# Spreading the queries by products, and drawing the scores by halves of the keys, in a fused convolution and attention kernel

## The chip, the cores and the metric

The kernel runs on one core of a Trainium2 chip. The metric is device time in microseconds (us), the median of three runs. A profile of one further execution shows every instruction, and its time stands beside its span below. The engines are TensorE (PE, matmuls; its weight loads are shown as PEld), VectorE (DVE), ScalarE (ACT), GpSimd (POOL) and SyncE (SP, which here only issues transfers). PSUM is the memory that PE writes, SBUF the working memory of the other engines, DRAM the large one outside.

## What is computed

Eight images of 32 x 32 places with 256 channels pass through two layers. Layer 0, cut to what matters here:

```python
conv_out = conv3x3(gn(x)) + conv_b                       # 192 of 256 channels
kqv = gn(x) @ qkv_w + qkv_b                              # k, q, v of 64 channels each, 8 heads of 8
logits = q @ k.T + rel_w(q, key_rel_w) + rel_h(q, key_rel_h)
weights = softmax(logits)                                # 1024 x 1024 per head
attn = (weights @ v) @ attn_w + attn_b                   # the other 64 channels
x = x + concatenate([conv_out, attn])
```

`rel_w` and `rel_h` add to each logit a number that depends on the query and on the distance of the key's column, or row, from the query's. Layer 1 is an attention over 1024 tokens (U = 128) with layer norm, and then a pair of experts for each image (a routed feed-forward network with gelu and a second norm).

## The kernel before

**Units.** Layer 0's attention of an image is worked in four units. A unit is one group of four heads (`g`) with one half of the 512 queries (`half`). For each unit the kernel builds a tile `F` in SBUF of 128 rows by 2 x 4 x 512 elements: for each half `a` of the keys, each head and each query, the features whose product with the key rows `KM` gives the whole logit, relative terms included. Rows 0 to 95 of `F` come from the DRAM scratch `fd` (the same for both `a`), 32 rows from the scratch `fy` (different for each `a`). Two further rows, `R_M` and `R_M + 32`, take the negated maxima in two parts, so that the logit less its maximum leaves PE ready for Exp.

A unit goes through `score` (32 products `lg` of 128 queries with 512 keys, each followed by a DVE maximum into `mx`), `fold`, `fold_in` and `fold_out` (the two halves' maxima become one, are transposed as `pmx`, and four ACT transfers `F<-mb` put them into F), `weigh` (32 products `st`, each followed by an Exp on ACT into `PT`) and `gather` (products `po` with the values). One `weigh` is a *place*; an image has 128 places, four units of 32. While unit n is weighed, the next unit is scored, paced by `starts`: for units 0 to 2 place p asks for p*4/3 + 1 scores, for unit 3, which scores the first unit of the next image, for (p - 5)*8/5 + 1. Place 25 folds, place 28 sends the maxima.

**Order around it.** The order on each engine is the order in which the program is written (`manual_schedule`); each engine works in that order. Other work is threaded in by `Fill`: `chains` are generators that move one step (to their next `yield None`) at each place, and `dense` holds the convolution's products `pc`, sent at the rate that `pace` gives: work still owed over the places left until place 88 of the image whose convolution runs (`LAST`). `second_layer(b - 1)` stands between units 0 and 1 of image b, `project(b - 1)` as a chain in unit 0.

**The path to a next image's first F.** `normalise(b)` makes `kq`, and from it `kqh`: a rounded high part and the low rest. When `may_query` allows (unit 2's first place) it stores the keys' rows (`kd`), and `queries(b)` fills `qs`: for each group, rows of the high part twice and of the low part twice, by eight transfers from `kqh` on SP; four more store query rows into `fd`; POOL copies `qs` into `qx` with rows and columns of the image exchanged. `keys` loads the key rows into `KM`. Then the products for the values (`pvv`), five empty places, and `features`: four `column` and four `row` products (`prel`, eight matmuls each) with a high and a low part each, stored into `fd` (`store_columns`) and `fy`. `Unit(b, 0)` then asks SP for F: both `fd` loads first, then four `fy` loads. `qs`, `qx` and the rows' buffers lie in `scr`, which has the same slot as that unit's F. The next `Unit(b, 1)` is asked for at unit 3's first place. For image 0 the same path runs at the start with nothing beside it, `taps` (the convolution's weights) and the 32 scores of unit 0 behind it.

Lines that the steps touch: L561 (the eight transfers), L568 (query rows into `fd`), L573 (`qx`), L581 (`keys`), L484 to L500 (`pvv` and empty places), L612 and L634 (`prel` parts), L620 and L641 (stores), L712 to L719 (F), L725 (`score`), L765 (`F<-mb`), L845 (`aT`) and L865 (`ns`), L927 (`pace`), L941 (`starts`). Products through the counting helper all carry L133.

Of the kernel before, what the change touches and what calls it, by code (L numbers as in the profile page):

```python
# [38 lines left out]
def kernel(  # L39
# [72 lines left out]
    with ExitStack() as ph:  # L112
# [59 lines left out]
        brow = work.tile([1, 2 * CO], FP, tag="n", name="brow", bufs=2)[:, 0 : 4 * DK].rearrange("p (a o) -> p a o", a=2)  # L172
        nc.scalar.dma_start(out=brow[:, 0], in_=qkv_b[0 : 2 * DK].rearrange("(o p) -> o p", o=1))
        M = 2 * HH - 1
        rawt = {}
        for n, table in (("h", key_rel_h), ("w", key_rel_w)):
            rawt[n] = wp.tile([M, DH], FP, tag=f"raw{n}", name=f"raw{n}")
            nc.scalar.dma_start(out=rawt[n], in_=table)
# [4 lines left out]
        nc.scalar.dma_start(out=l0b[:, 0, CO:C], in_=attn_b.partition_broadcast(P))  # L183
        rawc = f_tile("rawc", 2, FP).rearrange("p a h s -> p (a h s)")[:, 0 : 9 * KC * CO]
        nc.sync.dma_start(
# [7 lines left out]
        bo = wp.tile([P, 1, C], FP, tag="bo", name="bo")  # L193

        kqs = wp.tile([P, 1], FP, tag="kqs", name="kqs")
        nc.gpsimd.memset(kqs[0:DK, :], 1.0)
        nc.gpsimd.memset(kqs[DK : 2 * DK, :], DH**-0.5)
        gsel = wp.tile([P, P // GSIZE], FP, tag="gsel", name="gsel")
        nc.vector.tensor_reduce(gsel, ident.rearrange("p (g d) -> p g d", d=GSIZE), AX.X, ALU.add)
# [4 lines left out]
        gavg = gavg.rearrange("p g d -> p (g d)")  # L204
        hsel = wp.tile([P, HG], FP, tag="hsel", name="hsel")
        nc.vector.tensor_reduce(hsel, ident.rearrange("p (c h) -> p h c", h=HG), AX.X, ALU.add)
# [196 lines left out]
        def normalise(b):  # L403
# [70 lines left out]
            nc.sync.dma_start(out=kds[b % 2].rearrange("l p s -> p l s"), in_=kqb_[0:DK])  # L474
            qs, qx, scr = queries(b)
            if b == 0:
                for g in range(NG):
                    keys(b, g, nc.scalar)
            else:
                keys(b, 0)  # L480
            for g in range(2):
                nc.gpsimd.tensor_tensor(T[b][g], T[b][g], l0b.to_broadcast([P, 4, C]), ALU.add)
            v0[b] = work.tile([P, NT, DK], FP, tag="v0", name="v0")
            for g in range(2):  # L484
# [13 lines left out]
                yield None  # L498
            for _ in range(5):
                yield None  # L500
            yield from features(b, qs, qx, scr)
            units[b, 0] = Unit(b, 0)
            while b > 0 and (done[b - 1] < NT or not may_combine.get(b)):
                yield None
            yield from combine(b, base)

        may_query, may_combine, units = {}, {}, {}
        v0 = {}

# [43 lines left out]

        def queries(b):
            kqb_ = ready.pop(b)
            scr = f_tile("scr", b % 2).rearrange("p w h s -> p (w h s)")
            qs = scr[:, 0 : 2 * S].rearrange("p (g s) -> p g s", g=NG)
            qx = scr[:, 2 * S : 4 * S].rearrange("p (g s) -> p g s", g=NG)
            for i in range(4):
                for g in range(NG):  # L560
                    nc.sync.dma_start(  # L561
                        out=qs.bitcast(FP)[32 * i : 32 * i + 32, g],
                        in_=kqb_[DK + 32 * g : DK + 32 * g + 32, i // 2, :],
                    )
            fd = fds[b % 2]
            for g in range(NG):
                for c in range(2):
                    nc.sync.dma_start(  # L568
                        out=fd[g].rearrange("(l c p) s -> c p l s", c=2, p=32)[c, :, 0:2],
                        in_=kqb_[DK + 32 * g : DK + 32 * g + 32],  # L570
                    )
            for g in range(NG):
                nc.gpsimd.tensor_copy(  # L573
                    qx[:, g].rearrange("p (x y) -> p y x", y=HH), qs[:, g].rearrange("p (y x) -> p y x", x=WW)
                )
            return qs, qx, scr

# [8 lines left out]
        def features(b, qs, qx, scr):  # L586
# [49 lines left out]

            def store_columns():
                for g in range(NG):
                    dst = fds[b % 2][g][R_M * HG : (R_M + 64) * HG].rearrange("(l p) s -> p l s", p=P)
                    for p in (slice(HG, 64), slice(64, P)):  # L640
                        nc.sync.dma_start(out=dst[p], in_=whole[g].bitcast(FP)[p])  # L641

# [3 lines left out]
            for q in range(3):  # L646
                row(q)
                yield None
            yield None
            store_columns()  # L650
            yield None
# [50 lines left out]
        class Unit:  # L702


            def __init__(self, b, n):
                self.g, self.half = divmod(n, 2)
                g, cols = self.g, slice(self.half * 512, self.half * 512 + 512)
                self.F = f_tile("F", 2 if n == 3 else (b + n) % 2)
                self.Fb = self.F.bitcast(FP)
                fd = fds[b % 2][g].rearrange("(r h) s -> r h s", h=HG)  # L710
                for a in range(2):
                    nc.sync.dma_start(out=self.Fb[0 : R_M + 64, a], in_=fd[:, :, cols])  # L712
                for l in range(2):
                    r = R_Y + 16 * l
                    for a in range(2):
                        nc.sync.dma_start(
                            out=self.Fb[r : r + 16, a],
                            in_=fys[b % 2][g][l, 64 * a : 64 * a + 64, cols].rearrange("(i h) s -> i h s", h=HG),
                        )  # L719
                self.mx = work.tile([P, 2, 4, HG], FP, tag="mx", name="mx", bufs=2)  # L720
                self.scored = self.gathered = 0
                self.pts = {}
                self.po = None

            def score(self):  # L725

                n, a = divmod(self.scored, 2)
                i, hl = divmod(n, HG)
# [107 lines left out]
        def project(b, sec, half, gaps):  # L836
# [6 lines left out]
            for j, t in enumerate(ts):  # L843
                te.transpose(tp[0:DK, j * P : (j + 1) * P], at[:, t, :], ident)
            aT = work.tile([DK, 512], FP, tag="aT", name="aT")  # L845
            nc.scalar.copy(aT, tp[0:DK])
# [15 lines left out]
            for _ in range(gaps[1]):  # L862
                yield None

            ns = pt_tile("n")[:, 0 : 4 * C].rearrange("p (j c) -> p j c", c=C)  # L865

# [56 lines left out]
        def pace(b, place):  # L923

            left = (LAST if done.get(b, NT) < NT else 128 + LAST) - place  # L927
            return fill.owed / max(left, 1)
# [8 lines left out]
        def first_layer(b):  # L937


            more = b + 1 < B  # L940
            starts = [lambda p: p * 4 // 3 + 1] * 3 + [lambda p: (p - 5) * 8 // 5 + 1]  # L941
            for s in range(NU * NT):
# [29 lines left out]
                for p in range(HG):  # L972
                    place = 4 * j + p
                    unit.weigh(j, p)
                    if nxt in units:
                        u = units[nxt]
                        while u.scored < min(32, starts[n](place)):
                            u.score()
# [494 lines left out]
```

## Time and profile before

| | us |
|---|---|
| median of 3 runs (2437.92 to 2442.56) | 2438.52 |
| the profiled execution | 2442.88 |
| its span | 2441.1 |
| PE busy in the span | 2179.2 |
| DVE busy | 1406.7 |
| ACT busy | 1031.7 |
| first score | 94.65 |
| first `weigh` of image 0 | 131.26 |
| first `weigh` of image 7 | 1668.17 |
| first experts' matmul | about 1972 |

How to read it: the span has a start of 131 us, eight images of about 227 us each (some 102 of them in unit 0 with the second layer, and 41 to 44 in each other unit), an end of the second layer for the last image, and from about 1956 us the experts, which the change does not touch. An instruction's line gives its start and length; in square brackets is the engine's idle time before it and what ended it. `SPq` and `ACTq` are the issues of transfers by these engines.

### The profile page before, as it was taken

The numbers are of one execution on the slowest core, as the hardware profiler recorded it, in microseconds if no ns is written. First come the engines' busy times: TensorE is split into PE (matmuls) and PEld (weight loads), VectorE is DVE, ScalarE is ACT, GpSimd is POOL, SyncE is SP. The second block draws the span as 40 slices with busy tenths as digits, with TensorE's granted clock in tenths as the row PEclk, the third lists the DMA queues.
The fourth block names the chain that finished last, engine by engine and source line by source line (L and its number), as shares of the span: only waits on it lengthen the run. The fifth ranks groups of instructions, "written<-read, shape, count | busy, mean of one in ns | idle before, by whom it ended". The sixth has DMA issues, their size and how long they took to land.

```text
span 2441.1 us, 28659 instructions
## 1 busy us (share of the span) xinstructions
PE 2179.2 (89%) x10507; PEld 1402.5 (57%) x10507; DVE 1406.7 (58%) x3141; ACT 1031.7 (42%) x1969; POOL 501.9 (21%) x430
## 2 busy tenths in 40 slices
PE   4579899989999999899899999989997789999998
PEld 3446456645655665566456555655653556666665
DVE  4647657665767577567657675767571533333333
ACT  1135443554455445545543554455364322222332
POOL 2211220212031122302120311032011042222220
PEclk7689999999999999999999999999998989999999
DMA  4624512441371255025512532370120121121210
GB/s 115 148 66 93 129 36 70 121 79 36 78 173 19 44 113 138 11 65 123 116 36 70 141 59 44 75 176 10 44 44 1 51 93 70 69 69 69 79 51 26
DMA packets 92317, 185.97 MB, mean 76 GB/s; under 512 B 9441, under 2 KB 37994, under 8 KB 90642
## 3 DMA queue, kind: packets, MB, share of 16 engines
q1 hardware_dynamic: 90368, 181.55, 30.8%
q10 hardware_dynamic: 1810, 2.59, 0.5%
q8 instruction: 84, 1.38, 0.3%
q14 instruction: 55, 0.45, 0.1%
HBM read 112.15 MB, written 62.52 MB: 72 GB/s over the span
## 4 chain that ended last, share of the span: by engine, by line
PE 68%; DVE 16%; DMA 7%; ACT 5%; issue 2%; SPq 1%; ACTq 1%; POOL 1%; DVEq 0%; POOLq 0%
PE po L133 12%; PE phd L1383 9%; PE py L1400 9%; PE lg L133 9%; PE st L133 8%; DVE mx L738 6%; PE pc L133 5%; DMA F<-fy 3%; PE pq L133 3%; PE prel L133 2%; DMA F<-mb 2%; PE tp L137 2%; ACT PT L782 2%; PE pa L133 1%; PE pv L133 1%
## 5 line engine op out<-in xcount | busy, mean ns | idle before, releaser
L738 DVE TENSOR_REDUCE mx<-lg 128x1 f32<-128x512 f32 x1024 | 657.2, 683 | 282.8 <-PE lg L133 274.9
L782 ACT ACTIVATE PT<-st 128x512 f32<-128x512 f32 x1024 | 596.2, 598 | 474.8 <-PE st L133 426.4
L133 PE MATMUL st<-F,KM 128*128 128x512 f32 x1024 | 518.7, 510 | 46.6 <-ACT PT L782 30.6
L133 PE MATMUL lg<-KM,F 128*128 128x512 f32 x1024 | 384.0, 414 | 59.8 <-DMA F<-fy 49.3
L133 PEld LDWEIGHTS st<-F,KM 128*128 128x128 f32 x1024 | 196.6, 193 | 263.3 <-ACT PT L782 195.4
L133 PE MATMUL po<-PT,vk 128*32 128x512 f32 x2048 | 281.9, 621 | 0.0
L133 PE MATMUL pc<-convw,V 128*128 128x192 f32 x1152 | 264.0, 335 | 6.7 <-ACT mm L681 5.7
L133 PEld LDWEIGHTS lg<-KM,F 128*128 128x128 f32 x1024 | 196.3, 192 | 102.4 <-issue 58.1
L133 PEld LDWEIGHTS pc<-convw,V 128*128 128x128 f32 x1152 | 214.2, 196 | 48.5 <-issue 11.9
L1383 PE MATMUL phd<-n2T,w 128*128 128x512 f32 x512 | 225.4, 596 | 0.0
L1400 PE MATMUL py<-w,hT 128*128 128x256 f32 x1024 | 223.6, 379 | 0.0
L1400 PEld LDWEIGHTS py<-w,hT 128*128 128x128 f32 x1024 | 194.6, 190 | 33.3 <-issue 7.7
L1407 DVE TENSOR_TENSOR r<-py,n 128x256 f32<-128x256 f32 x64 | 27.2, 424 | 259.8 <-PE py L1400 259.8
L1383 PEld LDWEIGHTS phd<-n2T,w 128*128 128x128 f32 x512 | 96.2, 191 | 114.1 <-issue 110.4
L687 POOL TENSOR_TENSOR ms<-mm 128x192 f32<-128x192 f32 x32 | 19.1, 598 | 665.2 <-ACT mm L681 665.2
L1018 DVE TENSOR_REDUCE nm<-lg 128x1 f32<-128x512 f32 x128 | 85.8, 686 | 113.8 <-PE lg L133 113.8
L1022 ACT ACTIVATE pr<-lg,nm 128x512 f32<-128x512 f32 x128 | 86.8, 683 | 128.8 <-DVE nm L1019 128.6
L1390 ACT ACTIVATE hT<-phd,b1c 128x512 f32<-128x512 f32 x128 | 86.3, 686 | 96.6 <-PE phd L1383 96.4
L133 PE MATMUL lg<-nqk 128*128 128x512 f32 x256 | 120.8, 595 | 0.0
L133 PE MATMUL po<-pt,v 128*128 128x256 f32 x512 | 115.8, 379 | 0.0
L133 PEld LDWEIGHTS po<-pt,v 128*128 128x128 f32 x512 | 95.1, 190 | 11.6
L1343 POOL TENSOR_SCALAR w<-w,wbc 128x1024 f32<-128x1024 f32 x16 | 45.9, 2871 | 251.1 <-DMA w<-in_L_ffn_W_dram 249.3
(251 smaller groups left out, 2459.5 us busy)
## 6 DMA issues: line engine op xcount, KB each, us to landing
F<-fd SPq DMA_DIRECT2D x64, 768.0 KB
F<-fy SPq DMA_DIRECT2D x128, 128.0 KB
w<-in_L_ffn_W_dram SPq DMA_DIRECT2D x32, 512.0 KB
fy<-scr SPq DMA_DIRECT2D x48, 256.0 KB
T<-in_x_dram SPq DMA_DIRECT2D x16, 512.0 KB
scr<-kqh SPq DMA_DIRECT2D x64, 128.0 KB
fd<-kqh SPq DMA_DIRECT2D x32, 256.0 KB
fd<-rel SPq DMA_DIRECT2D x16, 512.0 KB
```

The lines of the kernel that those rows point to most:

```text
L133: nc.tensor.matmul(out, **kw)
L137: nc.tensor.transpose(out, in_, ident)
L687: nc.gpsimd.tensor_tensor(ms, mm[:, 0], mm[:, 1], ALU.add)
L738: nc.vector.tensor_reduce(self.mx[:, a, i, hl : hl + 1], lg, AX.X, ALU.max, negate=True)
L782: nc.scalar.activation(self.pts[j][:, hl, :], st, AF.Exp)
L1018: nc.vector.tensor_reduce(nm[:, h : h + 1], lg[h], AX.X, ALU.max, negate=True)
L1022: nc.scalar.activation(pr[:, h * 512 : (h + 1) * 512], lg[h], AF.Exp, bias=nm[:, 2:3], scale=scale, accum_out=rs[:, h, i : i + 1],)
L1343: nc.gpsimd.tensor_scalar(w2t, w2t, wbc[:, n : n + 1], None, ALU.mult)
L1383: nc.tensor.matmul(phd, lhsT=ws[k][0][:, kc, f * P : (f + 1) * P], rhs=n2T[:, kc, q * 512 : (q + 1) * 512], start=kc == 0, stop=kc == KC - 1,)
L1390: nc.scalar.activation(hT[:, k * NF + f, :], phd, AF.Gelu, bias=b1c[:, f, k * B + b : k * B + b + 1])
L1400: nc.tensor.matmul(py, lhsT=hT[:, k * NF + f, j * P : (j + 1) * P], rhs=ws[k][1][:, f, :], start=k + f == 0, stop=k == TOPK - 1 and f == N ...
L1407: nc.vector.tensor_tensor(r[:, j, :], py, n2[:, q * 4 + j, :], ALU.add)
```

## The change

The eight transfers that spread the queries' rows are replaced by PE products. A constant `twice` (128 x 192) holds for each of the two groups' 32 rows two identity blocks in columns 64 to 127 and zero elsewhere; used from column 64 it puts the high part into output rows 0 to 63, used from column 0 it puts the low part into rows 64 to 127, both summed in one PSUM tile `pqs`. ACT copies `pqs` into `qs`. `queries` becomes a generator of two steps, and its stores into `fd` come ahead of the products. `pvv` moves into `values`, which for image 0 runs after its first unit's F is asked for, and for the others after `queries`; the five empty places become one. For image 0 the column stores go to ACT's queue after row 0, and the keys' loads come, also on ACT, after F is asked for.

F is asked for by halves of the keys (`fd` and two `fy` loads for `a = 0`, then the same for `a = 1`), and `score` draws all 16 products of the first half ahead of the second's. Unit 3's scores are paced as those of the other units. For the last image `pace` spreads the convolution until place 120. Four small constants and the tables' raw rows move into free space of `rawc`, and `aT` into the `pt` slot that `ns` takes later, so that slot is taken from the start of `project`.

```diff
+        twice = wp.tile([P, 192], FR, tag="twice", name="twice")
+        for c in (0, 64):
+            nc.vector.tensor_scalar(twice[:, c : c + P], ident, 0.0, None, ALU.mult)
+        for g in range(NG):
+            r = slice(DK + 32 * g, DK + 32 * g + 32)
+            for i in range(2):
+                nc.vector.tensor_copy(twice[r, 64 + 32 * i : 96 + 32 * i], ident[r, r])
...
-            qs, qx, scr = queries(b)
-            if b == 0:
-                for g in range(NG):
-                    keys(b, g, nc.scalar)
-            else:
-                keys(b, 0)
+            yield from queries(b)
+            qs, qx, scr = spread.pop(b)
+            if b > 0:
+                keys(b, 0)
             for g in range(2):
                 nc.gpsimd.tensor_tensor(T[b][g], T[b][g], l0b.to_broadcast([P, 4, C]), ALU.add)
-            v0[b] = work.tile([P, NT, DK], FP, tag="v0", name="v0")
...
-            for _ in range(5):
-                yield None
+            if b > 0:
+                yield from values(b, base)
+                yield None
             yield from features(b, qs, qx, scr)
             units[b, 0] = Unit(b, 0)
+            if b == 0:
+                for g in range(NG):
+                    keys(b, g, nc.scalar)
+                yield None
+                yield from values(b, base)
...
-            for i in range(4):
-                for g in range(NG):
-                    nc.sync.dma_start(
-                        out=qs.bitcast(FP)[32 * i : 32 * i + 32, g],
-                        in_=kqb_[DK + 32 * g : DK + 32 * g + 32, i // 2, :],
-                    )
...
+                for q in range(2):
+                    c = slice(q * 512, q * 512 + 512)
+                    pq = lg_tile("pqs")
+                    for l in range(2):
+                        te.matmul(
+                            pq,
+                            lhsT=twice[r, 64 - 64 * l : 192 - 64 * l],
+                            rhs=kqh[r, l, c],
+                            start=l == 0,
+                            stop=l == 1,
+                        )
+                    nc.scalar.copy(qs[:, g, c], pq)
+                yield None
                 nc.gpsimd.tensor_copy(
                     qx[:, g].rearrange("p (x y) -> p y x", y=HH), qs[:, g].rearrange("p (y x) -> p y x", x=WW)
                 )
...
-            yield None
-            store_columns()
+                if b == 0 and q == 0:
+                    store_columns(nc.scalar)
+            yield None
+            if b > 0:
+                store_columns()
...
                 for a in range(2):
                     nc.sync.dma_start(out=self.Fb[0 : R_M + 64, a], in_=fd[:, :, cols])
-                for l in range(2):
-                    r = R_Y + 16 * l
-                    for a in range(2):
+                    for l in range(2):
+                        r = R_Y + 16 * l
                         nc.sync.dma_start(
...
-                n, a = divmod(self.scored, 2)
+                a, n = divmod(self.scored, 16)
...
-            aT = work.tile([DK, 512], FP, tag="aT", name="aT")
+            nt = pt_tile("n")
+            aT, ns = nt[0:DK, 1024:1536], nt[:, 0 : 4 * C].rearrange("p (j c) -> p j c", c=C)
...
-            left = (LAST if done.get(b, NT) < NT else 128 + LAST) - place
+            left = (120 if b + 1 == B else LAST if done.get(b, NT) < NT else 128 + LAST) - place
...
-            starts = [lambda p: p * 4 // 3 + 1] * 3 + [lambda p: (p - 5) * 8 // 5 + 1]
...
-                        while u.scored < min(32, starts[n](place)):
+                        while u.scored < min(32, place * 4 // 3 + 1):
```

More of the change, by code (lines that the diff above doesn't have):

```diff
@@ L173 @@
         nc.scalar.dma_start(out=brow[:, 0], in_=qkv_b[0 : 2 * DK].rearrange("(o p) -> o p", o=1))
+        raw = f_tile("rawc", 2, FP).rearrange("p a h s -> p (a h s)")
+        rawc, raw = raw[:, 0 : 9 * KC * CO], raw[:, 9 * KC * CO :]
         M = 2 * HH - 1
         rawt = {}
-        for n, table in (("h", key_rel_h), ("w", key_rel_w)):
-            rawt[n] = wp.tile([M, DH], FP, tag=f"raw{n}", name=f"raw{n}")
+        for i, (n, table) in enumerate((("h", key_rel_h), ("w", key_rel_w))):
+            rawt[n] = raw[0:M, i * DH : i * DH + DH]
             nc.scalar.dma_start(out=rawt[n], in_=table)
@@ L183 @@
         nc.scalar.dma_start(out=l0b[:, 0, CO:C], in_=attn_b.partition_broadcast(P))
-        rawc = f_tile("rawc", 2, FP).rearrange("p a h s -> p (a h s)")[:, 0 : 9 * KC * CO]
         nc.sync.dma_start(
@@ L197 @@
         nc.gpsimd.memset(kqs[DK : 2 * DK, :], DH**-0.5)
-        gsel = wp.tile([P, P // GSIZE], FP, tag="gsel", name="gsel")
+        gsel = raw[:, 32 : 32 + P // GSIZE]
         nc.vector.tensor_reduce(gsel, ident.rearrange("p (g d) -> p g d", d=GSIZE), AX.X, ALU.add)
@@ L204 @@
         gavg = gavg.rearrange("p g d -> p (g d)")
-        hsel = wp.tile([P, HG], FP, tag="hsel", name="hsel")
+        hsel = raw[:, 64 : 64 + HG]
         nc.vector.tensor_reduce(hsel, ident.rearrange("p (c h) -> p h c", h=HG), AX.X, ALU.add)
@@ L474, in normalise @@
             nc.sync.dma_start(out=kds[b % 2].rearrange("l p s -> p l s"), in_=kqb_[0:DK])
-            qs, qx, scr = queries(b)
+            yield from queries(b)
+            qs, qx, scr = spread.pop(b)
+            if b > 0:
+                keys(b, 0)
+            for g in range(2):
+                nc.gpsimd.tensor_tensor(T[b][g], T[b][g], l0b.to_broadcast([P, 4, C]), ALU.add)
+            if b > 0:
+                yield from values(b, base)
+                yield None
+            yield from features(b, qs, qx, scr)
+            units[b, 0] = Unit(b, 0)
             if b == 0:
@@ L478, in normalise, with values @@
                     keys(b, g, nc.scalar)
-            else:
-                keys(b, 0)
-            for g in range(2):
-                nc.gpsimd.tensor_tensor(T[b][g], T[b][g], l0b.to_broadcast([P, 4, C]), ALU.add)
+                yield None
+                yield from values(b, base)
+            while b > 0 and (done[b - 1] < NT or not may_combine.get(b)):
+                yield None
+            yield from combine(b, base)
+        may_query, may_combine, units = {}, {}, {}
+        v0, spread = {}, {}
+        def values(b, base):
             v0[b] = work.tile([P, NT, DK], FP, tag="v0", name="v0")
@@ L498, in normalise @@
                 yield None
-            for _ in range(5):
-                yield None
-            yield from features(b, qs, qx, scr)
-            units[b, 0] = Unit(b, 0)
-            while b > 0 and (done[b - 1] < NT or not may_combine.get(b)):
-                yield None
-            yield from combine(b, base)
-        may_query, may_combine, units = {}, {}, {}
-        v0 = {}
         def combine(b, base):
@@ L555, in queries @@
             kqb_ = ready.pop(b)
+            kqh = kqb_.bitcast(FR)
             scr = f_tile("scr", b % 2).rearrange("p w h s -> p (w h s)")
@@ L558, in queries @@
             qx = scr[:, 2 * S : 4 * S].rearrange("p (g s) -> p g s", g=NG)
-            for i in range(4):
-                for g in range(NG):
-                    nc.sync.dma_start(
-                        out=qs.bitcast(FP)[32 * i : 32 * i + 32, g],
-                        in_=kqb_[DK + 32 * g : DK + 32 * g + 32, i // 2, :],
-                    )
+            spread[b] = qs, qx, scr
             fd = fds[b % 2]
             for g in range(NG):
+                r = slice(DK + 32 * g, DK + 32 * g + 32)
                 for c in range(2):
@@ L569, in queries @@
                         out=fd[g].rearrange("(l c p) s -> c p l s", c=2, p=32)[c, :, 0:2],
-                        in_=kqb_[DK + 32 * g : DK + 32 * g + 32],
+                        in_=kqb_[r],
                     )
             for g in range(NG):
+                r = slice(DK + 32 * g, DK + 32 * g + 32)
+                for q in range(2):
[11 more added lines that the diff above has]
+                yield None
                 nc.gpsimd.tensor_copy(
@@ L575, in queries @@
                 )
-            return qs, qx, scr
         def keys(b, g, queue=nc.sync):
@@ L635, in column, with store_columns @@
                     fill.later(lambda ps=ps, hi=hi, lo=lo: nc.vector.tensor_tensor(lo, ps, hi, ALU.subtract) and None)
-            def store_columns():
+            def store_columns(queue=nc.sync):
                 for g in range(NG):
@@ L640, in store_columns @@
                     for p in (slice(HG, 64), slice(64, P)):
-                        nc.sync.dma_start(out=dst[p], in_=whole[g].bitcast(FP)[p])
+                        queue.dma_start(out=dst[p], in_=whole[g].bitcast(FP)[p])
             for q in range(4):
@@ L863, in project @@
                 yield None
-            ns = pt_tile("n")[:, 0 : 4 * C].rearrange("p (j c) -> p j c", c=C)
             def norm(q):
```

## The prediction

> **What bounds the kernel now.** I read the shares of the engines and of the chain that ended last, then TensorE's (PE's) waits, then the timeline of the start and of one image boundary, then busy time by stretch. First the page's busy time and chain by engine, and two lines of PE's waits (us in total, times, longest):
>
> ```profile
> PE 2179.2 (89%) x10507; PEld 1402.5 (57%) x10507; DVE 1406.7 (58%) x3141; ACT 1031.7 (42%) x1969; POOL 501.9 (21%) x430
> ...
> PE 68%; DVE 16%; DMA 7%; ACT 5%; issue 2%; SPq 1%; ACTq 1%; POOL 1%; DVEq 0%; POOLq 0%
> ...
> PE lg L133 <- DMA F<-fy: 49.3, 7, 26.9
> ...
> PE st L133 <- DMA F<-mb: 15.6, 9, 2.7
> ```
>
> PE is the bound; what can be won is where it stands: 49.3 us before scores (lg) until F is loaded. The start, in the timeline (start, length, idle before and who ended it):
>
> ```profile
> 35.09 6.38 SPq L561 DMA_DIRECT2D scr<-kqh  x8
> ...
> 50.10 3.69 POOL L573 CAST scr<-scr 128x1024 fp32r<-128x1024 f32 x2 [15.79 <-DMA scr<-kqh]
> ...
> 53.85 7.04 PE L133 MATMUL prel<-scr,tw 128*128 128x64 f32 x32 [19.65 <-POOL scr L573]
> ...
> 68.33 5.31 SPq L641 DMA_DIRECT2D fd<-rel  x4
> ...
> 81.06 1.28 SPq L712 DMA_DIRECT2D F<-fd  x2
> ...
> 94.65 2.47 PE L133 MATMUL lg<-KM,F 128*128 128x512 f32 x5 [26.94 <-DMA F<-fy]
> ...
> 178.63 0.76 PE L133 MATMUL lg<-KM,F 128*128 128x512 f32 x1 [10.41 <-DMA F<-fy]
> ```
>
> The row transfers take from 35.1 to 50; POOL turns the rows; features; stores; F asked for at 81.06 and there at 94.65. The last line is image 0's third unit, whose F cannot be asked for before unit 0 ends. Now the boundary between units 2 and 3 of image 1:
>
> ```profile
> 446.58 6.36 SPq L561 DMA_DIRECT2D scr<-kqh  x8
> ...
> 458.46 1.08 PE L133 MATMUL prel<-scr,tw 128*128 128x64 f32 x8 [0.38 <-POOL scr L573]
> ...
> 486.10 1.55 SPq L712 DMA_DIRECT2D F<-fd  x2
> ...
> 486.67 1.75 ACTq L765 DMA_DIRECT2D F<-mb  x3
> ...
> 492.80 0.47 PE L133 MATMUL st<-F,KM 128*128 128x512 f32 x1 [2.69 <-DMA F<-mb]
> ...
> 500.49 0.47 PE L133 MATMUL lg<-KM,F 128*128 128x512 f32 x1 [1.24 <-DMA F<-fy]
> ```
>
> Unit 3's four rows of maxima (mb) travel while the next image's F does; the first five of its places last from 489.6 to 500.5. Then busy time by stretch (PE, PEld, DVE, ACT, POOL, PE clock, DMA share, GB/s):
>
> ```profile
> 81.00:95.00 14.00, 0.35 (x1) 0.29 (x1) 0.00 (x0) 0.00 (x0) 0.00 (x0) 0.50 0.93 175
> ...
> 489.60:501.00 11.40, 7.21 (x30) 3.70 (x33) 3.39 (x7) 4.42 (x8) 4.56 (x7) 0.85 1.06 199
> 501.00:531.00 30.00, 27.18 (x143) 15.64 (x141) 24.41 (x42) 15.06 (x26) 3.89 (x5) 1.00 0.29 53
> ...
> 1833.00:1857.00 24.00, 21.06 (x99) 6.93 (x100) 0.55 (x2) 17.33 (x32) 0.00 (x0) 1.00 0.00 1
> ```
>
> While F travels the DMA engines are full; afterwards VectorE (DVE) carries 32 maxima in 27 places. In the chain from 501 to 525 DVE's maxima alternate with PE, and the last six (3.71 us) and the fold stand alone before pmx.
>
> **The change, part by part** (against the profiled 2441.1 us span; that run took 2442.9, the median of the runs is 2438.5, so I subtract from the median).
>
> *Setup.* Six DVE instructions for `twice` stand ahead of gavg. Neighbours there take 0.16 to 0.28 us when POOL's memsets do not hold them; with gsel, gavg and hsel pushed behind those memsets I add 1.7 us (bounds 1.0 and 2.9, the latter 2.7 for a held gavg row). DVE's weight copies, PE's pkb and the first transposes queue behind, so all of it reaches kqh: 34.3 becomes 36.0.
>
> *Queries at the start.* Eight matmuls at half clock, 0.43 us each (twice the 0.23 that two scores in a row take in the chain), four ACT copies of 0.59 and POOL's turn of 1.85 per group, in a pipeline: 36.0 + 0.9 + 0.6 + 0.9 + 0.6 for group 0 (copies done 38.6), POOL until 42.4. The features start at 42.5 instead of 53.85.
>
> *Features and stores at the start.* Columns 4 x 1.7 = 6.9 us, to 49.4; row 0 copied at 51.8. Now ACT issues four column stores (5.31 us by SP's row); rows 1 to 3, three SP stores and the keys' loads queue behind them on ACT. Row 1 is copied at 57.7 and stored; row 3 shares its buffer, so it waits for that store (2.15 us before): 61.5. Its own store lands some 3 us later, 64.6, and F's loads are released, 16.5 us earlier than 81.06. Half of F is 1 MB of the 2 MB that take 13.6 us: 5.5 to 6.8 alone. But the keys (1 MB, ACT, from 61.6) now travel too, in place of long before: from 531.0 to 537.5, with two key loads alone, the engines are 0.54 busy, 3.5 us for 512 KB, so 7 us for all. Score 1 comes between 64.6 + 6.8 = 71.4, if F goes first, and 64.6 + 6.8 + 7 = 78.4, if the keys do. Two queues share full engines: I take the middle, 75. Gain 94.65 - 75 = 19.6. The pvv products, which stood at 30.5 in PE's wait, now follow the first scores: 3.68 us, of which DVE's pace of 0.6 to 0.7 us a score hides some; +2.1. Net **-17.5** (-10 to -25).
>
> [...]
>
> *F in halves, first half drawn first.* The same bytes and matmuls; only where F is late does it count. Image 0's third unit: the wait of 10.41 is halved, **-5** (-3 to -6). Units whose F lies ready: 0.
>
> *Queries in the steady images (seven times).* The eight SP issues (6.36 us) go, the fd stores move ahead of them, and fd and the keys no longer wait behind a slot of F. PE pays 8 x 0.23 = 1.9 us (upper bound 8 x 0.645 = 5.2, the mean of the pk row); no row has a 32-row product, lg is the nearest. Unit 2 has 1.5 us of PE idle in 43, so nothing hides it: **+2.0**. ACT's 4 x 0.59 = 2.4 us are hidden by its 24.4 busy in 44; without that cover, Exp would pass them on. The first features come two places earlier in PE's order, 1.4 us earlier after those products, so F's loads start at about 484.7.
>
> [...]
>
> *Maxima spread over unit 3 (seven times).* Place 96 falls at 491.6. The mb rows still travel beside F, one about every 2 us as between 492.8 and 497.05, so places 96 to 100 remain slow, but six scores run in them, and F's first half should be there near 492 (486.10 + half of 14.4 - 1.4). The remaining 27 places carry 26 scores instead of 32: the DVE stretch and the lone 3.71 us shrink to PE's pace, 0.97 a place where image 7 scores at 1.33 a place (32 places from 1801.9 to 1832.9): 26 instead of 30.5 us. That is -4.5, and the queries' +2.0 is set against it: **-2.5 an image, -17.5** (per image +1 to -6; a gain is excluded only if place 96 waits longer).
>
> *Rest.* aT moves into a slot of pt: PT takes two of three slots at a time and frees one three places before it is needed, so 0; without that spare, an Exp would wait for POOL's 2.37 us at L886 twice an image. Image 7's conv spread to place 120: eight pc (0.19 each) leave PE-bound places for the 24 us in which ACT needs 17.3: **-1** (0 to -2).
>
> Sum: -17.5 - 5 - 17.5 - 1 = -41; 2438.5 - 41 = **2397.5**.
>
> **Rivals.**
> 1. *The queries' products eat unit 3's gain.* For it: unit 2 is PE-bound; mb sets places 96 to 100 either way. Against: the DVE maxima in the chain. Per image 0: -23.5, 2415.
> 2. *Unit 3 wins more.* If the earlier F lets mb through and the half clock (0.85 in that stretch) goes, 6 an image: -65.5, 2373.
> 3. *The start does not do what it says.* ACT's issues and the keys' loads put score 1 at 85: 10 less, 2407.5. For it the full engines; against it 16.5 us of earlier release.
> 4. *Slower.* PE works in order, and it now meets the first score at place 96, not 101. If the first half lands later than PE is ready, st, po and Exp of all places behind it stand. Each us costs 7; -41 is used up at 5.9 us an image, which means the half landing where F landed before, near 500. At 8 us: +15, 2453. For it: engines at 1.06 in that stretch. Against: half the bytes, asked for first.
>
> **Chances.** The forecast 0.54; rival 1 0.20, rival 2 0.08, rival 3 0.09, rival 4 0.09 (a part of it ends near zero). A measurement can tell 0.2% (4.9 us) from no change. Faster: 0.87, same 0.04, slower 0.09. Forecast alone 2385 to 2410; the range reaches to rival 1 and toward rival 2: 2380 to 2424.
>
> **What would show it.** Right: prel starts near 42.5 and score 1 near 75; image 0's third unit waits about 5 us; pqs rows of 8 per image at 0.23 spacing; units 3 about 36 us instead of 41.4, units 2 2 us longer; no lone run of six maxima before pmx. Wrong: a wait of lg for F at place 96 in every image (rival 4), Exp waiting for POOL L886's line, or score 1 past 80.

## The result, and the profile after

| | us |
|---|---|
| after, median of 20 runs | 2454.7 |
| before, median of 20 runs beside them | 2441.8 |
| ratio, with its 95% interval | 1.0051 (1.0035 to 1.0067) |
| span of the profiled execution, before and after | 2441.1, 2454.3 |

The change made the kernel 0.5% slower, where 41 us less were forecast. Nineteen of its twenty runs lie between 2440.9 and 2468.8 us, before's between 2436.7 and 2446.3: the new kernel is not only slower, it also varies three times as much. (The twentieth, 2483.1 us, was an execution in the slower state, with a granted clock of 0.94, and does not enter the ratio.) The spread is a first hint, and the products alone do not account for it: two kernels of experiment 5 that have them too (2411.4 and 2402.05 us) vary by 6.3 and 6.1 us in four runs each.

The page of after, busy time and chain by engine:

```profile
PE 2221.6 (91%) x10571; PEld 1429.6 (58%) x10571; DVE 1400.1 (57%) x3147; ACT 1049.2 (43%) x2001; POOL 497.8 (20%) x430
...
PE 71%; DVE 16%; ACT 5%; DMA 5%; ACTq 2%; issue 2%; POOL 1%; SPq 0%; DVEq 0%; POOLq 0%
```

PE is busy 42.4 us longer for 64 products more. By the rows further below (four of them take 1.43 to 2.07 us) these are 23 to 33 us, so other products have become slower as well. In the chain ACTq (ACT issuing transfers) has gone from 1% to 2%. PE's waits (us in total, times, longest) point the same way; first one of before, then after's:

```profile
PE st L133 <- ACT PT L782: 30.6, 53, 1.2
```

```profile
PE st L133 <- ACT PT L810: 43.1, 53, 2.6
PE lg L133 <- DMA F<-fy: 38.5, 3, 29.3
...
PE st L133 <- DMA F<-mb: 10.3, 6, 2.2
```

The wait for F, which the change was to shorten, fell from 49.3 to 38.5 us. But PE now waits 43.1 us for Exp, and up to 2.6 us at a time; before it was 30.6 us in as many waits of at most 1.2. Where does the time stand? The lengths of the units, from first `weigh` to first `weigh`, taken from the traces (images 1 to 6 as sums, minus before's):

| | before | after, minus before | stores moved back (below), minus before | best version (below), minus before |
|---|---|---|---|---|
| until the first `weigh` | 131.3 | -5.1 | -6.2 | -21.9 |
| image 0 | 170.4 | -6.5 | -4.9 | -1.9 |
| units 0, images 1-6 | 607.1 | -2.0 | -3.1 | -4.9 |
| units 1 | 252.5 | **+11.4** | -0.2 | -1.0 |
| units 2 | 256.6 | **+51.1** | +32.4 | +27.2 |
| units 3 | 250.3 | -38.7 | -38.7 | -34.4 |
| image 7 | 189.4 | +5.3 | +4.1 | -0.9 |
| rest | 583.6 | -2.2 | +0.2 | -1.2 |

Units 3 won 6.4 us each. Units 2, forecast at +2.0, lost 8.5 each, and the ends of units 1 another 1.9. (10.3 us of the difference between units 2 and 3 only change sides: PE now waits for unit 3's rows of maxima ahead of its first `weigh`, the third line of the waits above, and waited within unit 3 before.) The timeline of that boundary in image 1, first before (start, length, engine, operation; in brackets the idle time before and who ended it):

```profile
440.38 0.60 SPq L474 DMA_DIRECT2D kd<-kqh  x1
...
443.14 2.21 ACTq L765 DMA_DIRECT2D F<-mb  x4
...
445.40 1.09 ACT L782 ACTIVATE PT<-st 128x512 f32<-128x512 f32 x2 [1.74 <-DMA F<-mb]
446.05 0.19 PEld L133 LDWEIGHTS st<-F,KM 128*128 128x128 f32 x1 [0.61 <-ACT PT L782]
446.05 0.99 PE L133 MATMUL st<-F,KM 128*128 128x512 f32 x2 [0.32 <-ACT PT L782]
```

and after:

```profile
429.88 0.60 SPq L482 DMA_DIRECT2D kd<-kqh  x1
...
430.52 4.96 SPq L581 DMA_DIRECT2D fd<-kqh  x4
...
432.70 4.16 ACTq L793 DMA_DIRECT2D F<-mb  x4
...
436.90 1.09 ACT L810 ACTIVATE PT<-st 128x512 f32<-128x512 f32 x2 [3.74 <-DMA F<-mb]
...
437.56 1.28 PE L133 MATMUL st<-F,KM 128*128 128x512 f32 x2 [2.65 <-ACT PT L810]
...
439.19 2.07 PE L133 MATMUL pqs<-kqh,twice 32*128 32x512 f32 x4
...
444.21 1.43 PE L133 MATMUL pqs<-kqh,twice 32*128 32x512 f32 x4
```

Before, SP's queue held the eight `scr` transfers behind `kd`; they waited for a slot of F until 446.58, and the `fd` stores stood behind them. With the transfers gone, SP issues the `fd` stores at once, just when ACT issues unit 2's rows of maxima. These four issues take 4.16 us instead of 2.21, with the DMA engines 1.00 busy instead of 0.44 (experiment 2). The next Exp stands behind them in ACT's order (the profile names the last DMA event as releaser, but ACT itself is busy issuing until 436.86), and PE stands 2.65 us instead of 0.32. From 437.93 to 444.76 the granted clock is 0.50: the first four `pqs` take 2.07 us, the last four 1.43. In the chain of after the four issues stand one by one, here image 2's:

```profile
661.10 0.53 ACTq L793
661.67 1.04 ACTq L793
662.75 1.16 ACTq L793
663.95 1.35 ACTq L793
665.35 0.61 ACT PT L810
```

The half clock at the start of units 2 lasts 6.8 us in four images (units 2 of 49.4 to 49.9 us) and 17.1 and 20.5 in the two others (53.6 and 55.3). Image 0 is a control within the same run: there SP's four stores end at 201.1, ACT issues at 202.76 in 2.19 us, no half clock follows, and unit 2 is only 2.8 us longer than before.

### The profile page after: what moved, and what is told of

Its sections match the earlier page's. It is cut to its first block, busy times and chain, and to the rows that moved or that the text cites. A ratio compares the mean times of both kernels' runs of the same rounds, so it can differ in the third digit from the quotient of the medians.

```text
span 2454.3 us, 28751 instructions
## 1 busy us (share of the span) xinstructions
PE 2221.6 (91%) x10571; PEld 1429.6 (58%) x10571; DVE 1400.1 (57%) x3147; ACT 1049.2 (43%) x2001; POOL 497.8 (20%) x430
## 4 chain that ended last, share of the span: by engine, by line
PE 71%; DVE 16%; ACT 5%; DMA 5%; ACTq 2%; issue 2%; POOL 1%; SPq 0%; DVEq 0%; POOLq 0%
PE po L133 12%; PE lg L133 9%; PE phd L1409 9%; PE py L1426 9%; PE st L133 9%; DVE mx L766 5%; PE pc L133 5%; PE pq L133 3%; PE prel L133 2%; DMA F<-mb 2%; ACT PT L810 2%; PE tp L137 2%; PE pvv L133 1%; ACTq L793 1%; PE pa L133 1%
## 5 line engine op out<-in xcount | busy, mean ns | idle before, releaser
L133 PE MATMUL st<-F,KM 128*128 128x512 f32 x1024 | 521.2, 513 | 53.7 <-ACT PT L810 43.1
L133 PE MATMUL lg<-KM,F 128*128 128x512 f32 x1024 | 397.4, 421 | 48.1 <-DMA F<-fy 38.5
L1433 DVE TENSOR_TENSOR r<-py,n 128x256 f32<-128x256 f32 x64 | 27.2, 425 | 260.5 <-PE py L1426 260.5
```

The source lines that it names most:

```text
L133: nc.tensor.matmul(out, **kw)
L1433: nc.vector.tensor_tensor(r[:, j, :], py, n2[:, q * 4 + j, :], ALU.add)
```

## The experiments

**1. The stores behind the keys' loads, and the reverse of it in the kernel before.** Two kernels that move the same four instructions, one in each direction. First the changed kernel:

```diff
-            fd = fds[b % 2]        # in queries(), ahead of everything
-            for g in range(NG): ... nc.sync.dma_start(out=fd[g]..., in_=kqb_[r])
+            if b == 0:
+                store_queries()    # the same four stores
...
             if b > 0:
                 keys(b, 0)
+                store_queries()
```

> The changed kernel, with the four stores of the queries (fd) issued behind the keys' loads of the next image instead of ahead of them, images 1 to 7; products, copies and scoring as they are. Theory S (the stores, freed of the row transfers, are issued by SP while ACT issues the four rows of maxima, so these take 4.2 us instead of 2.2, Exp and PE stand 2.7 us and the clock falls): the rows of maxima take 2.2 us again, PE's wait for Exp there falls to 0.3-0.7 us, units 1 lose 1.5-2.5 us each, units 2 go from 49-55 us to 45-46.5 (42.8 plus the products' 2.9 us at 0.36 each), no half clock at the start of units 2; total 35 to 48 us less than the changed kernel, about 2407-2420. Rival P (the 32-row products and ACT's four copies in the middle of unit 2 cost the 7-12 us by themselves): units 2 stay at 49 or more, total within 10 us of 2454.7.

Measured: 2427.1 us, ratio to before 0.9945 (0.9914 to 0.9977), 27.6 us less than after (25.3 when each is set against the runs of before beside it). Its timeline:

```profile
430.51 2.21 ACTq L800 DMA_DIRECT2D F<-mb  x4
...
432.77 1.09 ACT L817 ACTIVATE PT<-st 128x512 f32<-128x512 f32 x2 [1.80 <-PE pc L133]
...
433.42 0.99 PE L133 MATMUL st<-F,KM 128*128 128x512 f32 x2 [0.71 <-ACT PT L817]
...
433.95 0.79 SPq L614 DMA_DIRECT2D KM<-kd  x2
...
434.78 3.37 SPq L584 DMA_DIRECT2D fd<-kqh  x4
```

The rows of maxima take 2.2 us again in every image, units 1 are back at 42, and five of the six units 2 run without a half clock, at 46.4 to 47.3 us. The whole gain is smaller than expected (2407 to 2420): in image 1 the clock still fell, for 17 us, after a stand of only 0.71 us, and units 2 are 4 us longer than before, not 2.9. Of these 4, the eight products take 2.2 (time from each PE start to the next), and most of the rest is a wait for the next rows of maxima (1.4 us in image 3) which now falls ahead of unit 3's first `weigh` and was counted in unit 3 before.

The kernel before with the four stores put ahead of the eight transfers, nothing else changed:

```diff
+            for part in (store_queries, spread_rows) if b > 0 else (spread_rows, store_queries):
+                part()
```

> The kernel before, with only the four fd stores issued ahead of the eight row transfers, images 1 to 7; no products, no other scoring. Theory S: the rows of maxima take 3.6-4.2 us, Exp waits for them 3.5 us or more instead of 1.74, units 1 gain about 2 us, units 2 go from 42.8 to 46-50 us with a half clock of 6.8 us or longer at their start; total 25 to 60 us more than before. Rival P: nothing changes but the order of SP's queue, within 5 us of before.

Measured: 2473.4 us, ratio 1.0140 (1.0103 to 1.0176), some 34 us more than before, without a product and without another order of scores:

```profile
438.31 5.09 SPq L571 DMA_DIRECT2D fd<-kqh  x4
...
440.48 4.10 ACTq L771 DMA_DIRECT2D F<-mb  x4
...
444.63 1.09 ACT L788 ACTIVATE PT<-st 128x512 f32<-128x512 f32 x2 [3.69 <-DMA F<-mb]
...
445.28 1.09 PE L133 MATMUL st<-F,KM 128*128 128x512 f32 x2 [2.26 <-ACT PT L788]
```

Rows of maxima of 4.0 to 4.1 us, units 1 longer by 1.4 to 2.6, units 2 at 45.6 to 51.1 in the five images whose clock fell and at 42.6, as in before, in the one where it did not, although PE stood 2.22 us there too. In that image the late rows cost only the 1.7 us at the end of unit 1; in the other five the half clock comes on top. The stores' place in the queue is the cause of the loss, shown from both sides; it needs no products.

**2. Two of the four stores ahead.** Is it SP's issuing that slows ACT's, or the data?

```diff
+            else:
+                store_queries((0,))      # two stores ahead
...
-                store_queries()
+                store_queries((1,))      # two behind the keys
```

> The changed kernel with two of the four fd stores behind the keys' loads and two left ahead, images 1 to 7. Their issue by SP then ends before ACT issues the rows of maxima, but their data are still on their way then. If what slows the rows of maxima is issuing beside SP's issue: rows of maxima 2.2-2.5 us, Exp's wait there 1.7-2.1, units 2 at 46-48. If it is the data on the engines: rows of maxima 3 us or more, Exp's wait 2.6 or more, units 2 at 48 or more in most images.

Measured: 2454.4 us, in one run, as much as after. The timeline, then busy time by stretch while the four rows are issued (PE, PEld, DVE, ACT, POOL, PE clock, DMA share, GB/s) in this kernel, and the same stretch in before and in after:

```profile
438.82 2.49 SPq L584 DMA_DIRECT2D fd<-kqh  x2
...
441.01 3.20 ACTq L802 DMA_DIRECT2D F<-mb  x4
...
444.90 0.99 PE L133 MATMUL st<-F,KM 128*128 128x512 f32 x2 [1.70 <-ACT PT L819]
```

```profile
441.00:444.30 3.30, 2.21 (x14) 0.97 (x13) 0.00 (x0) 0.51 (x2) 0.00 (x0) 1.00 0.87 219
```

```profile
443.10:445.40 2.30, 2.30 (x15) 1.11 (x14) 0.00 (x0) 0.56 (x2) 0.00 (x0) 1.00 0.44 96
```

```profile
432.70:436.90 4.20, 2.21 (x14) 0.97 (x13) 0.00 (x0) 0.46 (x1) 0.00 (x0) 1.00 1.00 233
202.70:205.00 2.30, 1.94 (x12) 0.64 (x11) 0.00 (x0) 0.52 (x1) 0.00 (x0) 1.00 0.46 110
```

SP's issue ends at 441.31, and still ACT's second and third row take 1.14 and 0.90 us; only the fourth is back at 0.52. With the DMA engines 0.44 to 0.46 busy the four take 2.2 us, at 0.87 3.2, at 1.00 4.16. Exp waits 2.79 us there, which lies on the side of the data in the expectation too. That speaks for the data on the engines and against the issuing, as far as one kernel can; image 0's row (0.46) fits it. Half the stores cost half the delay, but not half the price: PE's stand of 1.35 to 1.70 us brought 13.7 us of half clock in three of six images (units 2 of 53 us) and none in the others (47). Image 0 lost as much (13.7 us, unit 2 of 51.9) after a stand of 1.01 us beside undisturbed rows of maxima (2.20 us), so the total of this one run says little of what two stores cost.

**3. The third part alone.** The kernel before with F loaded and scored by halves and unit 3's maxima spread.

```diff
-                n, a = divmod(self.scored, 2)
+                a, n = divmod(self.scored, 16)
...
-                        while u.scored < min(32, starts[n](place)):
+                        while u.scored < min(32, place * 4 // 3 + 1):
```

> The kernel before with the third part alone: the first half of F asked for and scored first, and unit 3's maxima spread over the whole unit; queries by transfers, start as before. Theory T (the maxima in 27 places of unit 3 are what costs, as in the prediction): units 3 go from 41.4-43.4 to 35-37 us, units 2 stay at 42.5-43.5, image 0's second unit loses 2-3 us; total 35 to 48 us less than before, 2392-2405. Rival W (PE, in order, meets the first score at the unit's first place and stands until F's first half is there, because without the products the features and F come later): a wait of 3 us or more for F at the first score of each image, units 3 at 39 us or more, total within 20 us of before.

Measured: 2418.7 us, ratio 0.9890 (0.9866 to 0.9914). Rival W was right on the units: units 3 stay at 40.5 to 42.2 us, since PE now meets the first score at their first places and stands there 4.3 to 6.3 us:

```profile
938.03 0.76 PE L133 MATMUL lg<-KM,F 128*128 128x512 f32 x1 [6.31 <-DMA F<-fy]
```

On the total neither theory was right: against before, run beside it, it is 27 us less. The profiled run, the slowest of four, shows 18.7 of them, most of it elsewhere: 5.8 us at the start (first score 88.85 instead of 94.65, half of F being enough), 3.3 in image 0, 7 in all units of images 1 to 6 together, of which 2.6 in units 3. So spreading the maxima does not pay while PE stands at place 96 for F's first half.

**4. Transfers back in images 1 to 7, products in image 0 alone.** The five empty places ahead of the features come back with them.

```diff
             if b > 0:
                 yield from values(b, base)
-                yield None
+                for _ in range(5):
+                    yield None
...
+            if b > 0:
+                (the eight transfers of before)
             (the four fd stores)
             for g in range(NG):
+                if b == 0:
                     (products and copies)
```

> The changed kernel with the eight transfers of the queries back in images 1 to 7 (products in image 0 only), in their old place ahead of the fd stores. Theory T: units 2 go from 49-55 to 42.5-43.5 us (no products, no late rows of maxima), units 1 to 42, units 3 stay at 35-37; total 55 to 75 us less than the changed kernel, 2380-2400. Rival P2 (the products were worth their price, since the features and F's loads come earlier with them): units 2 and 3 together no better than the 82 us that they take with the stores moved alone, total 2410 or more.

Measured: 2429.2 us, ratio 0.9937 (0.9914 to 0.9959). My theory missed by 29 us and its rival held: units 2 are at 42.4 to 43.3 as expected, but units 3 at 40.0 to 41.2 with the wait of experiment 3, 83.2 us for the pair. With products and stores behind (next experiment) the pair takes 82.1, before it took 84.5. So the products cost nothing on balance. They do not bring F earlier, though. Here is image 3 in this kernel, then in the next experiment's kernel with products; its unit 2 begins at 887.96 and at 877.12:

```profile
927.41 0.60 SPq L750 DMA_DIRECT2D F<-fd  x1
...
935.89 0.77 PE L133 MATMUL lg<-KM,F 128*128 128x512 f32 x1 [4.43 <-DMA F<-fy]
```

```profile
916.30 0.59 SPq L748 DMA_DIRECT2D F<-fd  x1
...
924.49 0.39 PE L133 MATMUL lg<-KM,F 128*128 128x512 f32 x1
```

F is asked for 39.5 and 39.2 us after unit 2's first `weigh`, and the first score comes 47.9 and 47.4 us after it. The empty places do not hide a difference: over images 1 to 6 the features begin 11.7 to 12.3 us after that `weigh` with transfers and at 12.2 with products. What differs is how PE passes the time: with transfers it reaches place 96 after 43.0 us and stands, with products after 47.1 us and need not.

**5. The start: row 3's buffer, then the order of the requests.** The start of after:

```profile
41.52 7.03 PE L133 MATMUL prel<-scr,tw 128*128 128x64 f32 x32 [3.17 <-POOL scr L600]
45.35 1.20 ACT L660 CAST rel<-prel 128x256 fp32r<-128x256 f32 x4 [6.39 <-DMA fd<-kqh]
...
50.37 4.67 ACTq L667 DMA_DIRECT2D fd<-rel  x4
...
65.36 0.59 ACT L638 CAST scr<-prel 128x512 fp32r<-128x512 f32 x1 [9.14 <-DMA fy<-scr]
65.38 9.81 ACTq L607 DMA_DIRECT2D KM<-kd  x4
...
75.05 0.63 SPq L741 DMA_DIRECT2D F<-fd  x1
...
84.71 0.76 PE L133 MATMUL lg<-KM,F 128*128 128x512 f32 x1 [29.33 <-DMA F<-fy]
...
85.27 3.51 PE L133 MATMUL pvv<-qkvw,base 128*128 128x64 f32 x16
```

The features start at 41.5 (42.5 in the forecast), but row 3's copy stands 9.14 us for row 1's store, which travels together with 2 MB of column stores. The first edit gives row 3 of image 0 a free PT buffer:

```diff
-                r = b_tile("rel", FR) if q == 2 else scr[...]
+                r = b_tile("rel", FR) if q == 2 else pt_tile("row3", FR)[:, 0:S] if b == 0 and q == 3 else scr[...]
```

> The changed kernel, with the fourth piece of the row features of image 0 in a buffer of its own (a free one of the PT's), so that its copy does not wait for the store of the second piece. Theory B (the shared buffer holds the start): the wait of 9.14 us ahead of the copy goes, the copy comes at 56-58 instead of 65.4, F is asked for at 66-68 instead of 75.05 and the first score comes at 76-78 instead of 84.71. Rival D (4 MB of stores fill the DMA engines from 51 to 67 whatever waits for what): the copy comes early, but F is asked for at 72 or later and the first score comes at 81 or later.

Measured, in one run: the copy comes at 55.73, F is asked for at 65.73, the first score at 78.16:

```profile
55.73 0.60 ACT L638 CAST row<-prel 128x512 fp32r<-128x512 f32 x1
...
65.73 0.63 SPq L741 DMA_DIRECT2D F<-fd  x1
...
78.16 0.77 PE L133 MATMUL lg<-KM,F 128*128 128x512 f32 x1 [23.08 <-DMA F<-fy]
```

6.5 of the 9.1 us came through, just outside the 76 to 78 of theory B. Next, with row 3's buffer kept, the keys are asked for ahead of the features and the values' products drawn ahead of the first score, and the pace goes back to 88; once with transfers (and five empty places) in images 1 to 7, once with products and the stores behind the keys:

```diff
             qs, qx, scr = spread.pop(b)
-            if b > 0:
+            if b == 0:
+                for g in range(NG):
+                    keys(b, g, nc.scalar)
+            else:
                 keys(b, 0)
...
             yield from features(b, qs, qx, scr)
+            if b == 0:
+                yield from values(b, base)
             units[b, 0] = Unit(b, 0)
```

> As the kernel with the transfers back, with the pace back at 88 and image 0's start eased: the fourth piece of the row features in a buffer of its own, the keys asked for right behind the queries' products (before the features) and the values' products ahead of the first score. Theory B (in the start the order of the requests counts: keys travel while the engines are idle from 46 to 50, F has the engines to itself, and the products of the values run while PE waits): keys landed by 50-52, first score at 70-74 instead of 84.7, first weighing 10-14 us earlier, image 7 another 5 us; total 14 to 20 us less than the kernel with the transfers back. Rival D (the stores and F are bound by the DMA engines alone): first score at 77 or later, 5 to 11 us less.

> The same ease of the start and the pace at 88, but with the products of the queries in all images and the fd stores behind the keys' loads. Theory T: as much less than the kernel with the stores moved alone as the other pair shows, 14 to 20 us, 2405-2413, and 20 to 35 us more than with the transfers, since the products cost unit 2 some 4 us an image. Rival P2: no slower than with the transfers.

Measured: 2413.0 us, ratio 0.9858 (0.9828 to 0.9887), and 2411.4, ratio 0.9868 (0.9843 to 0.9893). Both gains over their partners hold (16 us each; 19 for the second by the ratios), but with products the kernel is no slower than with transfers, as the rival said. The first scores, 76.6 and 77.8, miss the expected 70 to 74: the keys now travel beside the queries' stores (the engines' busy share from 40 to 46 is 1.11 in the version with transfers), and the first `rel` copy, whose buffer `kqh` these stores still read, waits 10.37 us for them in the version with transfers instead of 6.39. So in the last pair image 0's column features get a buffer of their own, and SP stores them ahead of the rows:

```diff
-                work.tile([P, 2, S], FR, tag="kqh", name="rel"),
+                work.tile(...) if b > 0 else pt_tile("rel", FR).rearrange("p (l s) -> p l s", l=2),
...
+            if b == 0:
+                store_columns()
             for q in range(3):
```

The version with transfers also lets unit 3's maxima begin three places later, to take PE's stand of experiment 3 away: `(place - 3) * 3 // 2 + 1`.

> The kernel with products in all images, stores behind the keys and the eased start, with the same two changes of image 0 (column features in a buffer of their own, stored by SP ahead of the rows). Theory B: first rel copy at 43-44 instead of 49, stores from 48 on, first score at 72-75 instead of 77.8, total 3-6 us less, 2404-2409. Rival D (4 MB of stores and 1 MB of F at the engines' rate, whatever the order): first score at 76 or later, no difference.

> The kernel with transfers in images 1 to 7 and the eased start, where unit 3's maxima begin three places later (places 99 to 120 of the image), and image 0's column features get a buffer of their own, stored by SP ahead of the rows. Theory T (with the transfers, what is left to win is PE's stand of 4-4.6 us for the first half of F at the first score): that stand falls to 0-1.5 us, no half clock of 6.8 us at unit 3, units 3 from 40.3 to 36-38; first score of the kernel at 71-74 instead of 76.58 (the first rel copy no longer waits for the queries' stores, 10.37 us); total 2383-2400. Rival M (the maxima in 22 places are DVE's again, 0.69 us each): units 3 at 39 or more, total 2402-2412.

Measured with products: 2402.05 us, ratio 0.9832 (0.9809 to 0.9855), 9 us less than the partner where 3 to 6 were expected. The first copy no longer waits for a transfer, F is asked for at 64.67, and the first score comes at 72.69, as theory B had it:

```profile
45.31 1.20 ACT L667 CAST rel<-prel 128x256 fp32r<-128x256 f32 x4 [6.48 <-PE prel L133]
...
64.67 0.64 SPq L748 DMA_DIRECT2D F<-fd  x1
...
72.69 2.47 PE L133 MATMUL lg<-KM,F 128*128 128x512 f32 x5 [10.27 <-DMA F<-fy]
```

With transfers: 2403.8, ratio 0.9844 (0.9823 to 0.9864), first score 73.25, no stand of over 1.1 us at a first score from image 2 on, yet units 3 only at 39.0 to 41.7, and the total is rival M's. Its mechanism (32 maxima in 22 places) is the smaller part of it: over the six units 3 PE stands 9.2 us for DVE (3.9 in its partner) and 14.5 us ahead of `weigh`s for the rows of maxima (none there), so that its idle time has only moved. Both versions beat before, run beside them, by 38 and 40 us, and so the change as well; they can't be told apart from each other.

**6. The pace of the last image.** After has a new wait in image 7's unit 0:

```profile
1777.57 1.01 PE L133 MATMUL pmean<-all,acc 128*128 128x1 f32 x4 [4.33 <-DVE acc L1162]
```

```diff
-            left = (120 if b + 1 == B else LAST if done.get(b, NT) < NT else 128 + LAST) - place
+            left = (LAST if done.get(b, NT) < NT else 128 + LAST) - place
```

> The changed kernel, with the planner's place for the last image's filling work back at 88 from 120. Theory L (the convolutions saved up for places past 88 are missing as filling work elsewhere in image 7, so that PE stands 4.3 us before pmean in its unit 0): image 7's unit 0 goes from 109.2 to 101-104 us, its four units together from 194.7 to 189-191, total 4-6 us less. Rival: the wait before pmean comes from the second layer's own order and stays, image 7's units together 193-196.

Measured, in one run: unit 0 of image 7 at 99.7 us instead of 109.2, the image at 188.8 instead of 194.7. Theory L holds; the total, 2453.4, hardly shows it, as in this run units 2 happened to have 72 us of half clock at their starts against 65 in the profile of after.

## Why the prediction was wrong

**The step that failed** is the one on the steady images: "the eight SP issues (6.36 us) go, the fd stores move ahead of them". It was costed at nothing, as a relief of SP's queue. It asked what the stores had waited for and not what they would meet: ACT's four rows of maxima, issued 2.8 us behind `kd` in before's timeline. Of the 54 us between forecast and result 39 lie in units 0 to 3 of images 1 to 6, 12 ahead of the first `weigh` and 6 in image 7 (image 0 and the rest give some 4 back). The price of the stores in the profile: 11.4 us in units 1 and 51.1 in units 2, less 13.2 for the products (6 x 2.2) and the 10.3 that changed sides, so 39 us over six images. Undoing it alone gave 25 to 28 us in the medians (in the profiled run with one half clock of 17 us left), doing it alone in the kernel before cost 34. With the stores behind, the change is 12 us faster than before.

What two queues cost each other when the engines are full was weighed at the start (the middle of 71.4 and 78.4) and not here. The runs give it a number: with the engines 0.99 to 1.01 busy instead of 0.44 ACT's issue itself grew from 0.52 us to between 1.04 and 1.36 for the second to fourth row.

**The queries' products** (+2.0): right in size. Eight take 2.2 us, 0.28 each at a granted clock of 0.99 (image 3 of experiment 1's first kernel); image 0's unit 2 grew by 2.8. (For the start the text writes 0.43 for twice 0.23, which is 0.46; nothing hangs on it.) What they buy was read wrongly: the first features were to come 1.4 us earlier and F's loads with them, but with products (where the clock did not fall) and with transfers alike F is asked for 39 to 40 us after unit 2's first `weigh`. The products fill time in which PE would stand at place 96.

**Unit 3's spread** (-4.5): right in the profile of after. The 38.7 us of units 3, less the 10.3 that changed sides, are 4.7 an image. Units 2 and 3 together, with the stores out of the way, win 1.0 to 2.4 us an image in the three profiles with products, so the forecast's 2.5 was somewhat high.

**Setup, features, image 0's third unit**: right. `kd` is issued from the finished `kqh` at 36.25 (36.0), the features start at 41.52 (42.5), the wait of 10.41 became 4.89 (half).

**The start** (-17.5): mis-sized; it was the third rival's 85. Row 3, behind row 1 in a shared buffer, was given 4 us and took 10 (row 1's store had 2 MB of columns beside it, the DMA engines 0.96 busy from 54 to 62), so it was copied at 65.36 instead of 61.5. Its own store was given some 3 us and took nearly 10: it was issued just behind ACT's loads of the keys (65.38), and SP stood 7.3 us for it (0.8 with row 3's buffer apart). So F was asked for at 75.05 instead of 64.6, and the score came at 84.71 instead of 75. Of the 9.9 us won, only 5.1 reach the first `weigh`: two blocks of `pvv`, 3.51 and 3.29 us at the granted clock of 0.50 that PE has from 85 to 92, stand between the first scores (3.68 us in all, less some hidden, in the forecast). With row 3's buffer apart and nothing else, F was asked for at 65.73 and the score came at 78.16, the late end of the forecast's 71.4 to 78.4; with the order of the requests and the columns' buffer changed too, at 64.67 and 72.69.

**The tail's pace** (-1): wrong in sign, +5.3. The convolutions kept back were the filling that had covered PE while DVE made `acc`.

**The fourth rival**, a stand at place 96, does not occur in images 1 to 6 of after; it does, with 2.5 to 6.3 us, in the kernels without the products that score unit 3 from its first place. That its 2453 us lie near the measured 2454.7 is chance.

## What to carry to other kernels

When transfers are taken out of a queue, what stood behind them starts earlier: look up what each other queue issues at that new time, and which engine waits in order behind those issues. A wait that looks useless can keep two stages' transfers apart: with it the rows of maxima took 2.2 us here, without it 4.0 to 4.2. A short stand of PE can cost more than its length: in after stands of 2.1 to 2.7 us were followed by units 2 that took 49 to 55 us, where 46.4 to 47.3 were enough without a half clock (experiment 1). So a wait of 2 us in front of a PE-bound stage is worth removing even where the stage has room, and when the runs of a kernel suddenly spread wider, such a stand is one thing to look for. Lastly, work that seems free may only fill a wait: look up what the wait is for before saying that the work shortens it.

## What the runs showed of the hardware

The granted clock fell after short stands of PE, and not always. At the boundary of units 1 and 2 a stand of 2.1 to 2.7 us was followed by a half clock in 11 of 12 images of two kernels, after and the kernel before with the stores ahead (6.8 us in seven, 13.7 to 20.5 in four, while PE was kept busy), and stands of 1.35 to 1.70 us, with two stores ahead, in three of six (13.7 us). With all stores behind the keys, the first kernel of experiment 1, one of six images had a half clock, of 17 us, after a stand of 0.71 us. A stand of 1.01 us in image 0 was followed by 13.7 us with two stores ahead and by none in after, and the stands of 0.31 to 0.36 us in images 0 to 6 of before by none in their units 2. (The runs of row 3's buffer alone and of the pace alone, whose stores stand as in after, add twelve images with stands of 2.1 to 2.4 us, all followed by a half clock of 3.4 to 20.5 us.) Between the first `weigh` and 1800 us the half clocks in the traces of before and after last 3.41, 6.83, 10.24, 17.07 or 20.48 us, one to six times 3.41. What decides whether and for how long stays open.

An issue on ACT's queue was not a fixed cost: 0.52 to 0.54 us for each of the four rows of maxima with the DMA engines 0.44 busy (image 1 of before); with them 0.99 to 1.01 busy (images 1 to 6 of after) the first still took 0.52 to 0.53 and the others 1.04 to 1.36.
